# Causal masks of an attention with heads of 64: from mask matmuls to a masked maximum on VectorE and a select on GpSimd

## The chip, the cores and the metric

One core of one Trainium2 chip runs the whole program in a single launch. The metric is the device time of that launch in microseconds (us). The kernel before has three timed runs: 3772.35, 3780.45 and 3801.22 us, with a median of 3780.45. Apart from these, one execution was profiled, and every row of a profile in this document belongs to such an execution.

The engines are named as in the profile: PE is TensorE's matmuls, PEld its weight loads, DVE is VectorE, ACT is ScalarE, POOL is GpSimd, SP issues most of the DMAs.

## The reference

The program is four transformer layers on 2048 tokens of 128 channels, each of them half a feed-forward layer, an attention, and another half of the feed-forward layer. Attentions 0 and 3 are causal. The change is about attention 3: 16 heads of 64 over all 2048 tokens, keys and values made from a latent of 64, rotary embedding on queries and keys.

```python
q = jnp.einsum('bsd,qd->bsq', x, wq).reshape(B, S, H, D).transpose(0, 2, 1, 3)
kv_latent = jnp.einsum('bsd,ld->bsl', x, w_kv_down)
k = jnp.einsum('bsl,ql->bsq', kv_latent, w_k_up).reshape(B, S, H, D).transpose(0, 2, 1, 3)
v = jnp.einsum('bsl,ql->bsq', kv_latent, w_v_up).reshape(B, S, H, D).transpose(0, 2, 1, 3)
q = q * cos + _rotate_half(q) * sin
k = k * cos + _rotate_half(k) * sin
scores = jnp.einsum('bhsd,bhtd->bhst', q, k) / jnp.sqrt(jnp.float32(D))
causal = jnp.triu(jnp.full((S, S), -jnp.inf, dtype=jnp.float32), k=1)
scores = scores + causal[None, None]
probs = jax.nn.softmax(scores.astype(jnp.float32), axis=-1).astype(q.dtype)
out = jnp.einsum('bhst,bhtd->bhsd', probs, v)
```

Attention 0 has the same causal mask on 8 heads of 16, and matters here because it already carries its mask in the other way.

## The kernel before

All attentions run through one routine, `flash`. The 2048 tokens are four chunks of 512 (`CH`), each of four tiles of 128. Attention 3 takes its heads in pairs (`nh` is 2), so an iteration is one pair of heads and one chunk of queries, 8 pairs by 4 chunks, 32 iterations, in the order of `its`: all four chunks of a pair, then the next pair. A causal iteration of query chunk `qc` sees key chunks 0 to `qc`. The last of them is the diagonal one, and needs the mask.

An iteration has two passes, written as two generators.

- `stream_a` finds the maximum of every query's scores. For each tile `r` of 128 queries and each key chunk it multiplies queries by keys (L1045) for two heads into one double bank of PSUM (`first_pass_bank`, tag `s1`, two buffers), and VectorE reduces both halves in one `tensor_reduce` (L1068). On the diagonal chunk only `w` = 128, 256, 384 or 512 columns are made. The maxima are then put, negated, into rows of the query tile, so that the second pass's matmul subtracts them.
- `stream_b` makes the scores again, transposed, one tile of 128 keys against 512 queries at a time (L1150, two matmuls per head), ScalarE takes the exponential from PSUM into a tile `pt` in SBUF (L1159), and TensorE multiplies it by the values (`pv`, L1114). On the four diagonal key tiles the columns start at `c0` = 0, 128, 256 or 384, and the 128 columns from `c0` hold the triangle. The values of a key tile are emitted only after the scores of the next one, to give the exponential time. The first of these matmuls also waits for the last exponential by a manual dependency (`last_exp`), so that all the pair's exponentials are there.

How the sum of exponentials is made differs by attention. In attention 3 `on_exp` (L1965) adds every `pt` into a running sum for its head: the first head of the pair on GpSimd and the second on VectorE, and both on VectorE for the last two key tiles of an iteration. After the iteration, ones are multiplied by the sums (L1978), and the inverse travels through DRAM to scale the output (L1994, L2008).

The order of the work on TensorE is written out by hand. `pe(...)` keeps its matmuls in program order, and the main loop of `flash` decides after every yielded piece of `stream_b` how far `stream_a` may be ahead, counted in columns (`leads`, `knots`). So the maxima of coming iterations lie between the exponentials and values of the present one. `fill` adds pieces of the projections of coming pairs in between: TensorE products (L227 to L229, L1698, L1699), rotary products on VectorE (L1734) and rotary additions on GpSimd (L1744, L1750). VectorE and GpSimd have in-order queues whose order a scheduler sets; the reductions of the first pass have high priority in it.

The mask. `tiled` is true in the attentions whose heads are packed into strips of the array (0, 1 and 2), and false in attention 3. Where it is true and the attention is causal (attention 0), L1060 adds a strip, 384 columns of zeros and then the triangle, in the instruction that takes the maximum, and L1161 zeroes the triangle of `pt` with a select on GpSimd. Where it is false (attention 3), a matmul of the identity by a triangle of -1e30 in bfloat16 adds the mask into PSUM: L1049 in the first pass (`maskq_b`) and L1155 in the second (`maskk_b`).

```python
masked = last and not tiled
...
if masked:
    pe(nc.tensor.matmul(
        ps[:, o + w - P : o + w], masks_b["ident_b"],
        masks_b["maskq_b"], start=False, stop=True,
    ))
```

Of the kernel before, what the change touches and what calls it, by code (L numbers as in the profile page):

```python
# [9 lines left out]
F32 = mybir.dt.float32  # L10
# [17 lines left out]
E = 8  # L28
# [20 lines left out]
    (COLS, [("rb1", 4), ("rb2", 4), ("eb1", 4 * E), ("ln_scale", 1), ("ln_bias", 1),  # L49
            ("w1_s", 4), ("w2_s", 4), ("h1_s", 4), ("h2_s", 4), ("hscale", 1)]),  # L50
    (ROWS, [("rb3", E), ("b_proj", C), ("bias2", C), ("w3_s", C)]),
    (CONSTS, [("ident", P), ("before", P), ("maskq", P), ("maskk", P), ("least", E * E),
              ("ecap", TC * E), ("iota", P), ("iotaj", NJ), ("tile", NC * 2 * TC), ("spare", NJ), ("tok", 1),
              ("geo", P)]),
)
# [9 lines left out]
def tile_macaron(ctx: ExitStack, tc: tile.TileContext, a: dict, out: bass.AP, stages=STAGES):  # L65
# [35 lines left out]
    def cs(name):  # L101
        return cst[:, slice(*CONSTS[name])]
# [99 lines left out]

    def make_constants(other):
        for name, src in (
            ("ident_b", ident), ("maskq_b", cs("maskq")), ("maskk_b", cs("maskk")),
            ("before_b", cs("before")), ("ones_b", ones),
        ):
            masks_b[name] = const.tile([P, P], BF16, name=name)
            in_order(nc.vector.tensor_copy(masks_b[name], src), other)
        masks_b["ident_r"] = const.tile([P, P], F32R, name="ident_r")  # L210
        in_order(nc.vector.tensor_copy(masks_b["ident_r"], ident), other)
# [758 lines left out]
    def flash(io, pool, early, its, nh, causal, scale, s1, s2, pv_mm, put_max, begin, finish, poll=None,  # L970
# [20 lines left out]
        def pe(ins):  # L991
            return tc.keep_in_program_order(ins)
# [4 lines left out]
        def chunks(qc):  # L997
            return qc + 1 if causal else NC

        if tiled and causal:  # L1000
            junk = pool.tile([P, CH], F32, name="junk")
            strip = pool.tile([P, CH], F32, name="strip")
            nc.gpsimd.memset(strip[:, : CH - P], 0.0)
            nc.vector.tensor_copy(strip[:, CH - P :], cs("maskq"))
# [20 lines left out]
        def stream_a():  # L1025
            for n, (g, qc) in enumerate(its):
                begin(n)
                nk = chunks(qc)
                npair = (nk + 1) // 2
                mp = pool.tile([P, TC, nh, NC], F32, name="mp", tag="mp", bufs=3)  # L1030
                for pi in range(npair):
                    for r in range(TC):
                        before = hook(n, pi, r) if hook is not None else None
                        if pi == r == 0 and before is None:
                            before = last_top.get(n - 1)
                        for kc in range(2 * pi, min(2 * pi + 2, nk)):
                            for j0 in range(0, nh, 2):
                                ps = first_pass_bank()
                                last = causal and kc == qc
                                masked = last and not tiled  # L1040
                                w = (r + 1) * P if last else CH
                                for j in range(2):
                                    o = j * CH
                                    lhsT, rhs = s1(n, j0 + j, r, kc)
                                    pe(nc.tensor.matmul(  # L1045
                                        ps[:, o : o + w], lhsT, rhs[:, :w], start=True, stop=not masked
                                    ))
                                    if masked:
                                        pe(nc.tensor.matmul(  # L1049
                                            ps[:, o + w - P : o + w], masks_b["ident_b"],  # L1050
                                            masks_b["maskq_b"], start=False, stop=True,
                                        ))
                                    pos[0] += w
                                    if not tiled:
                                        yield w
                                both = ps.rearrange("p (j n) -> p j n", j=2)
                                with tc.high_priority():
                                    if last and tiled:
                                        for j in range(2):
                                            ins = nc.vector.tensor_tensor_reduce(  # L1060
                                                junk[:, :w], both[:, j, :w], strip[:, CH - w :], 1.0, NEG,
                                                ALU.add, ALU.max, mp[:, r, j0 + j, kc : kc + 1],
                                            )
                                            if before is not None:
                                                in_order(ins, before)
                                                before = None
                                    else:
                                        ins = nc.vector.tensor_reduce(  # L1068
                                            mp[:, r, j0 : j0 + 2, kc], both[:, :, :w], AX.X, ALU.max,
                                        )  # L1070
                                if before is not None:
                                    in_order(ins, before)
                                    before = None
                                if tiled:
                                    yield 2 * w
                mx = pool.tile([P, TC, nh], F32, name="mx", tag="mxa", bufs=3)
                nc.vector.tensor_reduce(mx, mp[:, :, :, :nk], AX.X, ALU.max, negate=True)
                put, last_top[n] = put_max(n, mx, pe)

                def done(n=n, put=put):  # L1080
                    put()
                    ready.add(n)

                after(2000.0, done)

        def stream_b():
# [45 lines left out]
            for n, (g, qc) in enumerate(its):  # L1132
# [5 lines left out]
                for kt in range(nt):  # L1138
                    at[1] = kt
                    c0 = CH - width(kt, qc)  # L1140
                    diag = causal and kt >= qc * TC
                    pts = {}
                    for at_j, j in enumerate(order):
                        if alive[0] or at_j % 2:
                            ps = bank("s2")
                        else:
                            ps = first_pass_bank()[:, :CH]
                        terms = s2(n, j, kt)
                        for i, (lhsT, rhs) in enumerate(terms):
                            pe(nc.tensor.matmul(  # L1150
                                ps[:, c0:], lhsT, rhs[:, c0:],
                                start=i == 0, stop=i == len(terms) - 1 and (tiled or not diag),
                            ))
                        if diag and not tiled:
                            pe(nc.tensor.matmul(  # L1155
                                ps[:, c0 : c0 + P], masks_b["ident_b"], masks_b["maskk_b"], start=False, stop=True
                            ))
                        pt = early.tile([P, CH], F32, name="pt", tag="pt", bufs=2 * nh + 2)
                        ex = nc.scalar.activation(pt[:, c0:], ps[:, c0:], AF.Exp, scale=scale)  # L1159
                        if diag and tiled:  # L1160
                            ex = nc.gpsimd.affine_select(  # L1161
                                pt[:, c0 : c0 + P], pt[:, c0 : c0 + P], [[1, P]], ALU.is_ge, 0.0,
                                base=0, channel_multiplier=-1,
                            )
                        pts[j] = pt
                        if on_exp is not None:
                            on_exp(n, kt, j, pts, c0)
                        if len(terms) > 1:
                            step((CH - c0) * (len(terms) - 1))
                        yield CH - c0  # L1170
                        if tiled and alive[0]:
                            if at_j % 2:
                                values(at_j // 2)
                        elif at_j == (split_at if alive[0] else nh - 1):
                            values()
                    if pv is None:
                        pv = held("pv")
                    pend[0] = (n, kt, nt, c0, pts, pv, ex)
                    if not alive[0]:
                        io.lead(2.3)  # L1180
# [940 lines left out]
def _constants():  # L2121
# [3 lines left out]
    def put(name, v):  # L2125
        c[:, slice(*CONSTS[name])] = v
# [2 lines left out]
    put("ident", np.eye(P))  # L2129
    put("before", i[:, None] < i[None, :])  # L2130
    put("maskq", np.where(i[None, :] > i[:, None], NEG, 0.0))
    put("maskk", np.where(i[:, None] > i[None, :], NEG, 0.0))
    e = np.arange(E)
    put("least", np.where(e[None, :] < e[:, None], 0.0, 2.0**-126).reshape(1, -1))
    put("ecap", np.tile(e * CAP - SLOTS - (P - 1) / 2.0, TC)[None, :])
# [130 lines left out]
```

## Time and profile before

| What | us |
|---|---|
| median of the timed runs (lowest, highest) | 3780.45 (3772.35, 3801.22) |
| profiled execution, device time | 3774.4 |
| its span in the trace | 3772.5 |
| attention 0, masked maxima on VectorE, first to last | 188.4 to 421.1 |
| attention 0, selects on GpSimd, first to last | 211.4 to 458.5 |
| attention 3, first to last mask matmul of the first pass | 2615.3 to 3586.4 |
| attention 3, first to last mask matmul of the second pass | 2637.5 to 3624.7 |
| PE busy in the span | 3463.1 |
| DVE busy in the span | 2858.9 |
| ACT busy in the span | 2075.1 |
| POOL busy in the span | 838.8 |

The device time and the span differ by 1.9 us, which lies around the span. The mean granted clock of TensorE over the span is 0.943 of full speed.

Matmul rows overlap each other: a row's length is the way of one matmul through the array, and the next begins before it ends. So busy time on PE says how long something was in the array, and what a matmul takes from the stream is read from the distance of two starts. A wait is put down to the releaser that came last. A chain of waits is followed back from the last instruction to what released it, and its shares say which lines the end of the program hung on.

### The profile page before, as it was taken

The page shows a single profiled execution, that of the slowest core. Times are in us where ns is not written, and L with a number is a line of the kernel's source. Part 1 is how long each engine was busy: PE and PEld are TensorE (multiplying, and loading weights), DVE is VectorE, ACT ScalarE, POOL GpSimd, SP SyncE. Part 2 cuts the span into 40 slices and gives each one's busy share as a digit, 9 for nine tenths or more (in the row PEclk, how much of TensorE's full clock was granted, in tenths as well). Part 3 has the DMA queues.
Part 4 walks back from the last instruction along what each step waited for, and adds up shares of the span by engine and source line. Part 5 has one row for each costly group of instructions (what it writes and reads, how often), then busy time and mean ns, then how long its engine had stood idle before and what let it go on. Part 6 is the DMA issues. An engine that isn't in the chain of part 4 may idle for free.

```text
span 3772.5 us, 61601 instructions
## 1 busy us (share of the span) xinstructions
PE 3463.1 (92%) x23613; PEld 1894.5 (50%) x23613; DVE 2858.9 (76%) x4794; ACT 2075.1 (55%) x3858; POOL 838.8 (22%) x860
## 2 busy tenths in 40 slices
PE   7689988978999999997999999888899999999999
PEld 5543366853333333883333333376455555555458
DVE  6578556768999996778899999654787777777762
ACT  3246732316888888331788888732344444444442
POOL 1511124010000000111000000144665444532341
PEclk9779989988999999995899999999999999999999
DMA  3410023000000000101000000013653343322110
GB/s 104 94 49 19 28 67 93 1 26 7 16 6 15 7 4 1 35 15 56 10 14 8 14 5 4 15 45 88 187 181 102 104 127 117 119 63 61 29 34 12
DMA packets 135015, 186.65 MB, mean 49 GB/s; under 512 B 27520, under 2 KB 54658, under 8 KB 134720
## 3 DMA queue, kind: packets, MB, share of 16 engines
q1 hardware_dynamic: 132160, 177.46, 15.9%
q0 software_dynamic: 2560, 5.25, 0.9%
q8 instruction: 186, 3.05, 0.3%
q14 instruction: 109, 0.89, 0.1%
HBM read 117.89 MB, written 45.87 MB: 43 GB/s over the span
## 4 chain that ended last, share of the span: by engine, by line
PE 68%; DVE 9%; ACT 4%; POOL 3%; issue 3%; DMA 2%; SPq 0%; DVEq 0%; POOLq 0%; ACTq 0%
PE pv L1114 21%; PE s L1150 20%; PE s L1045 4%; DVE mp L1068 4%; PE pd L725 3%; ACT pt L1159 2%; PE bank L227 2%; PE bank L228 2%; PE bank L229 2%; PE sums L1978 1%; PE bank L922 1%; PE pu L227 1%; PE pu L228 1%; PE py L2014 1%; PE pu L229 1%
## 5 line engine op out<-in xcount | busy, mean ns | idle before, releaser
L1159 ACT ACTIVATE pt<-s 128x512 f32<-128x512 f32 x3008 | 1552.4, 586 | 640.8 <-PE s L1150 401.6
L1068 DVE TENSOR_REDUCE mp<-s 128x2 f32<-128x1024 f32 (+3 forms) x1440 | 1630.1, 1183 | 161.8 <-PE s L1045 116.5
L1114 PE MATMUL pv<-pt,v 128*32 128x256 f32 (+5 forms) x9848 | 1053.8, 439 | 23.6 <-ACT ov L1528 11.3
L1150 PE MATMUL s<-q,km 32*128 32x512 f32 (+2 forms) x2368 | 746.9, 501 | 26.0 <-ACT pt L1159 16.3
L1045 PE MATMUL s<-km,qt 32*128 32x512 f32 (+3 forms) x2368 | 631.2, 517 | 55.4 <-DVE mp L1068 34.9
L1150 PEld LDWEIGHTS s<-q,km 32*128 32x128 f32 (+1 forms) x2368 | 328.4, 188 | 546.7 <-issue 352.0
L1114 PEld LDWEIGHTS pv<-pt,v 128*32 128x32 f32 (+1 forms) x9848 | 234.0, 112 | 394.1 <-issue 203.2
L143 POOL TENSOR_TENSOR rs<-rs,minus_half 128x4 f32<-128x4 f32 x56 | 58.7, 1048 | 1544.9 <-DVE rs L142 1544.1
L1150 PE MATMUL s<-q,k 128*128 128x512 f32 (+3 forms) x1280 | 387.3, 395 | 10.0 <-DVE rot L1734 7.0
L1150 PEld LDWEIGHTS s<-q,k 128*128 128x128 f32 x1280 | 210.8, 190 | 204.0 <-issue 100.1
L1965 DVE TENSOR_TENSOR sum<-sum,pt 128x512 f32<-128x512 f32 (+3 forms) x328 | 249.9, 772 | 81.2 <-ACT pt L1159 77.7
L1965 POOL TENSOR_TENSOR sum<-sum,pt 128x512 f32<-128x512 f32 (+1 forms) x200 | 260.0, 1300 | 217.6 <-ACT pt L1159 200.4
L1045 PEld LDWEIGHTS s<-km,qt 32*128 32x128 f32 (+1 forms) x2368 | 240.8, 195 | 118.1 <-DVE mp L1068 78.7
L1045 PE MATMUL s<-k,q 128*128 128x512 f32 (+3 forms) x640 | 237.5, 405 | 19.8 <-DVE mp L1068 15.7
L715 ACT ACTIVATE sg<-pg 128x1024 f32<-128x1024 f32 x72 | 73.9, 1027 | 174.4 <-PE pg L229 158.9
L1045 PEld LDWEIGHTS s<-k,q 128*128 128x128 f32 x640 | 124.0, 196 | 64.1 <-DVE mp L1068 23.2
L725 PEld LDWEIGHTS pd<-l1d,h 128*128 128x128 f32 x1152 | 139.3, 192 | 5.6
L725 PE MATMUL pd<-l1d,h 128*128 128x128 f32 x1152 | 140.1, 275 | 0.0
L717 DVE TENSOR_TENSOR h<-pu,sg 128x1024 f32<-128x1024 f32 x72 | 87.9, 1220 | 60.3 <-PE pu L229 55.3
L1734 DVE TENSOR_TENSOR rot<-rot,tab 128x512 f32<-128x512 f32 x128 | 87.4, 685 | 53.0 <-PE rot L1699 21.7
L1744 POOL TENSOR_TENSOR rot<-rot,rot 128x512 f32<-128x512 f32 x64 | 89.4, 1397 | 115.5 <-DVE rot L1734 101.4
L908 ACT ACTIVATE f<-bank,cols 128x512 f32<-128x512 f32 x64 | 44.1, 689 | 115.5 <-PE bank L229 109.5
(569 smaller groups left out, 4462.4 us busy)
## 6 DMA issues: line engine op xcount, KB each, us to landing
tab<-in_l3rope SPq DMA_DIRECT2D x66, 256.0 KB
q<-q SPq DMA_DIRECT2D x128, 128.0 KB
k<-k SPq DMA_DIRECT2D x64, 256.0 KB
l0e<-in_l0e SPq DMA_DIRECT2D x32, 256.0 KB
q<-h SPq DMA_DIRECT2D x32, 256.0 KB
q<-rot SPq DMA_DIRECT2D x32, 256.0 KB
k<-h SPq DMA_DIRECT2D x32, 256.0 KB
k<-rot SPq DMA_DIRECT2D x32, 256.0 KB
```

The source lines that it names most:

```text
L227: nc.tensor.matmul(ps, wh, xh, start=start, stop=False)
L228: nc.tensor.matmul(ps, wh, xl, start=False, stop=False)
L229: nc.tensor.matmul(ps, wl, xh, start=False, stop=stop)
L717: nc.vector.tensor_tensor(h.rearrange("p m n -> p (m n)"), pu, sg, ALU.mult)
L725: nc.tensor.matmul(pd[:, i, :], h[:, m, i * P : (i + 1) * P], wd[:, m, :], start=m == 0, stop=m == 1,)
L1045: pe(nc.tensor.matmul(ps[:, o : o + w], lhsT, rhs[:, :w], start=True, stop=not masked))
L1068: ins = nc.vector.tensor_reduce(mp[:, r, j0 : j0 + 2, kc], both[:, :, :w], AX.X, ALU.max,)
L1114: i = pe(nc.tensor.matmul(pv[out_rows, lo:hi], lhsT, pts[j][:, lo:hi], start=kt == 0, stop=kt == nt - 1 and hi == CH))
L1150: pe(nc.tensor.matmul(ps[:, c0:], lhsT, rhs[:, c0:], start=i == 0, stop=i == len(terms) - 1 and (tiled or not diag),))
L1159: ex = nc.scalar.activation(pt[:, c0:], ps[:, c0:], AF.Exp, scale=scale)
L1744: nc.gpsimd.tensor_tensor(f, f, halves[1].bitcast(F32), ALU.add)
L1965: eng.tensor_tensor(t[:, c0:], other[:, c0:], pts[j][:, c0:], ALU.add)
```

## The change

In every causal attention, attention 3 included, the diagonal chunk of the first pass is now reduced by one `tensor_tensor_reduce` per head (add the strip, take the maximum) in place of the mask matmul and the paired `tensor_reduce`, and the triangle of a diagonal `pt` is zeroed by GpSimd's `affine_select` after the exponential in place of the mask matmul before it. The values and the sums then depend on the select. The score matmuls close their own accumulation. The scratch output `junk` of the maximum becomes bfloat16 instead of float32, for attention 0 as well. The constant `maskk`, and the bfloat16 copies of both masks, are gone.

```diff
-    (CONSTS, [("ident", P), ("before", P), ("maskq", P), ("maskk", P), ("least", E * E),
+    (CONSTS, [("ident", P), ("before", P), ("maskq", P), ("least", E * E),
...
-            ("ident_b", ident), ("maskq_b", cs("maskq")), ("maskk_b", cs("maskk")),
+            ("ident_b", ident),
...
-        if tiled and causal:
-            junk = pool.tile([P, CH], F32, name="junk")
+        if causal:
+            junk = pool.tile([P, CH], BF16, name="junk")
             strip = pool.tile([P, CH], F32, name="strip")
             nc.gpsimd.memset(strip[:, : CH - P], 0.0)
             nc.vector.tensor_copy(strip[:, CH - P :], cs("maskq"))
...
-                                masked = last and not tiled
                                 w = (r + 1) * P if last else CH
...
-                                        ps[:, o : o + w], lhsT, rhs[:, :w], start=True, stop=not masked
+                                        ps[:, o : o + w], lhsT, rhs[:, :w], start=True, stop=True
                                     ))
-                                    if masked:
-                                        pe(nc.tensor.matmul(
-                                            ps[:, o + w - P : o + w], masks_b["ident_b"],
-                                            masks_b["maskq_b"], start=False, stop=True,
-                                        ))
...
-                                    if last and tiled:
+                                    if last:
                                         for j in range(2):
                                             ins = nc.vector.tensor_tensor_reduce(
                                                 junk[:, :w], both[:, j, :w], strip[:, CH - w :], 1.0, NEG,
...
-                                start=i == 0, stop=i == len(terms) - 1 and (tiled or not diag),
-                            ))
-                        if diag and not tiled:
-                            pe(nc.tensor.matmul(
-                                ps[:, c0 : c0 + P], masks_b["ident_b"], masks_b["maskk_b"], start=False, stop=True
+                                start=i == 0, stop=i == len(terms) - 1,
                             ))
                         pt = early.tile([P, CH], F32, name="pt", tag="pt", bufs=2 * nh + 2)
                         ex = nc.scalar.activation(pt[:, c0:], ps[:, c0:], AF.Exp, scale=scale)
-                        if diag and tiled:
+                        if diag:
                             ex = nc.gpsimd.affine_select(
                                 pt[:, c0 : c0 + P], pt[:, c0 : c0 + P], [[1, P]], ALU.is_ge, 0.0,
                                 base=0, channel_multiplier=-1,
                             )
...
-    put("maskk", np.where(i[:, None] > i[None, :], NEG, 0.0))
```

## The prediction

> **What bounds the kernel now.** I read the page first, then windows of each engine over the attention with 16 heads of 64 (2600 to 3640 us), the chain of waits there, the groups by shape, the waits, and a timeline of TensorE. Only that attention uses the edited branches; the earlier causal attention, 16 wide, already runs the new code and serves as a price list.
>
> From the page, then the chain of that stretch (shares of it), then three windows (pair of heads 4, query chunks 0 to 2 and chunk 3; pair 6, chunks 0 to 2; columns: length, PE, PEld, DVE, ACT, POOL busy, granted clock, DMA share, GB/s):
>
> ```profile
> PE 3463.1 (92%) x23613; PEld 1894.5 (50%) x23613; DVE 2858.9 (76%) x4794; ACT 2075.1 (55%) x3858; POOL 838.8 (22%) x860
> ...
> by line: PE s L1150 26.7%; PE pv L1114 23.7%; PE s L1045 12.2%; issue 4.9%; DVE mp L1068 3.3%; PE sums L1978 2.8%; PE py L2014 2.6%; DVE sum L1965 1.8%; PE s L1155 1.4%; PE rot L1698 1.4%; PE s L1049 1.3%; PE rot L227 1.2%; PE rot L229 1.1%
> ...
> 3183.00:3257.00 74.00, 72.57 (x365) 40.75 (x366) 59.49 (x88) 32.20 (x64) 30.82 (x25) 1.00 0.33 100
> 3257.00:3302.00 45.00, 45.00 (x210) 22.57 (x208) 34.15 (x49) 22.65 (x44) 28.45 (x21) 1.00 0.51 154
> 3414.00:3483.00 69.00, 67.43 (x343) 36.89 (x345) 50.36 (x78) 30.85 (x60) 18.11 (x15) 1.00 0.20 55
> ```
>
> See that TensorE is the bound at full granted clock, that the mask matmuls (L1049, L1155) are 2.7% of the chain of some 1040 us, so about 28 us, and that VectorE, 73 to 80% busy, is the runner-up: its maxima and sums already take 5.1%.
>
> The prices, groups by shape; L1060, L1161 and the accumulator read are from the 16-wide attention (190 to 480 us), the rest from 2640 to 3640 us (columns: count, busy us, mean ns, idle before, its releaser):
>
> ```profile
> L1155 PE MATMUL s<-maskk_b,ident_b 128*128 128x128 bf16 x255 | 58.7, 230 | 0.0
> L1049 PE MATMUL s<-maskq_b,ident_b 128*128 128x128 bf16 x240 | 53.9, 230 | 0.0
> L1068 DVE TENSOR_REDUCE mp<-s 128x2 f32<-128x1024 f32 x218 | 264.0, 1221 | 78.6 <-PE s L1045 68.3 <-PE s L1049 8.8
> L1068 DVE TENSOR_REDUCE mp<-s 128x2 f32<-128x256 f32 x30 | 12.3, 411 | 0.0
> L1060 DVE CUSTOM_DVE_ANT_0 junk<-s,strip 128x512 f32<-128x512 f32 x32 | 22.0, 688 | 3.9 <-PE s L1150 2.2 <-PE s L1045 0.3
> L1060 DVE DVE_READ_ACCUMULATOR2_ANT mp<- 128x1 f32 x126 | 10.4, 82 | 0.0
> L1060 DVE CUSTOM_DVE_ANT_0 junk<-s,strip 128x128 f32<-128x128 f32 x30 | 8.6, 286 | 1.0
> L1161 POOL TENSOR_SCALAR_AFFINE_SELECT pt<-pt 128x128 f32<-128x128 f32 x128 | 36.3, 294 | 190.4 <-ACT pt L1159 189.2
> L1965 POOL TENSOR_TENSOR sum<-sum,pt 128x512 f32<-128x512 f32 x168 | 226.0, 1345 | 173.8 <-ACT pt L1159 171.4
> L1965 DVE TENSOR_TENSOR sum<-sum,pt 128x512 f32<-128x512 f32 x168 | 171.9, 1023 | 45.3 <-ACT pt L1159 45.0
> ```
>
> A mask row's 230 ns is latency. What it takes from the stream is the distance between starts, in the timeline of TensorE (start, length):
>
> ```profile
> 3123.30 0.40 PE L1045 MATMUL s<-k,q 128*128 128x512 f32 x1
> 3123.54 0.23 PE L1049 MATMUL s<-maskq_b,ident_b 128*128 128x128 bf16 x1
> 3123.58 0.59 PE L1150 MATMUL s<-q,k 128*128 128x384 f32 x2
> ...
> 3133.63 0.23 PE L1049 MATMUL s<-maskq_b,ident_b 128*128 128x128 bf16 x1
> 3133.79 1.08 PE L1114 MATMUL pv<-pt,v 128*64 128x512 f32 x4
> ...
> 3215.14 0.39 PE L1045 MATMUL s<-k,q 128*128 128x512 f32 x1
> 3215.46 0.44 PE L1114 MATMUL pv<-pt,v 128*64 128x128 f32 x4
> ```
>
> A mask before a score matmul costs 0.04 us, before the values (pv) 0.16; without one, score to pv takes 0.32 where score, mask, pv takes 0.24 + 0.16 = 0.40.
>
> **The change, part by part.** 8 pairs of heads by 4 query chunks are 32 iterations, each with 8 masks in the first pass (4 row tiles, 2 heads) and 8 in the second (4 diagonal key tiles, 2 heads): 512 mask matmuls go, with their weight loads. 119 of them stand before a pv: 119 x 0.08 = 9 us. The other 393 at 0.04 to 0.05: 17 us. Sum 26 us, near the chain's 28. [...]
>
> Added on VectorE: each of 128 paired TENSOR_REDUCEs becomes two masked maxima with two accumulator reads. At 512 columns 2 x (0.688 + 0.082) = 1.54 against 1.22; at 128, 2 x (0.286 + 0.082) = 0.74 against 0.41; the two shapes between likewise. So 0.32 us more each, 128 x 0.32 = 41 us. Cover: VectorE's 20 to 27% of idle, and the first half can begin one score matmul earlier (0.24 us). Behind a longer maximum stand sums and the next maximum, and TensorE waits for the first-pass bank (two buffers). Of L1068's time the chain holds 3.3% of 1040 = 34 us out of 325 busy, a tenth; I put a fifth of 41 on the path: 8 us, ends 0 and 41.
>
> Added on GpSimd: 256 selects of 0.294 us, 75 us more where it is busy some 40 to 63%. The select stands between exponential and both users, pv and the sum. For pv I laid every diagonal exponential beside its pv in the trace: between the end of the second head's exponential and the pv start, medians are 3.2, 2.9, 1.5 and 1.5 us for the four diagonal tiles, and a quarter of the last have under 0.8 (least 0.05). A select needs some 0.5 us with handovers (my estimate; the traced select waits 0.1 or so for its ACT row), up to 1.3 us more behind a GpSimd sum. Shortfall: about 0.3 us on 16 of the last tiles and less on some others, near 5 us; another 5 for backlog, when GpSimd's head of queue holds a sum or rotary add that waits for VectorE (rows: 73.7 us waited for L2008 in 7 places, longest 18.5; they fall at key tile 1 of chunk 1, just ahead of its selects). 10 us, ends 2 and 40.
>
> The sums: 200 adds of diagonal tiles are on VectorE (the last two tiles always, the second head before). Setting max(end of exponential, end of the GpSimd instruction then running) plus 0.5 us against each add's traced start, VectorE would stand a further 90 us in all. Queued behind are maxima, and rotary products that GpSimd itself awaits. The chain holds 1.8% = 19 us of the sums' time, a fourteenth; waiting is less evenly buffered, so I take an eighth: 12 us, ends 0 and 90.
>
> [...]
>
> With one answer, zero: the strip's memset and copy (1 to 2 us on GpSimd and VectorE, ahead of a stage that opens with DMA waits; uncovered, +2); maskk's 64 KB and two casts at the start (beside loads of weights, -0.5 at most); the bfloat16 junk in the 16-wide attention (the input is still float32 in PSUM; between -5 and +5 for 128 rows); SP's queue and the order of TensorE's remaining work (unchanged in the text).
>
> Sum: -26 + 8 + 10 + 12 = +4 us on the profiled execution's 3774.4 (span 3772.5), 3778; that execution lies 6 below the median of 3780.45, so 3785 on the runs' scale.
>
> **The rivals.** *All cover holds.* Every addition hides in slack and only the masks' time shows: 3780 - 26 = 3754. For it: the medians of slack, VectorE's idle quarter. Against: TensorE already waits for L1068 and both cover engines are in order.
>
> *Convoy on VectorE.* Its adds wait for selects, selects stand behind 1.3 us GpSimd sums, and the maxima behind the adds leave TensorE without a first-pass bank. Place: the diagonal tiles of chunks 1 and 2, where maxima for the next chunk are made. Price: half of 90 + half of 41 + 20 for pv - 26 = +60, so 3840. It decides once 0.25 us or so of each add's wait reaches TensorE (200 x 0.25 = 50, with 8 + 10 - 26 = +42). For it: 101 waits of L1965 for an exponential exist already (79.0 us). Against: two banks and the idle quarter.
>
> *The masks were free.* If TensorE only waits elsewhere instead of 26 us saved, the additions stand alone: +10 to +30, 3800. For it: the page's PE ends are modelled; against: the chain counts the masks.
>
> **How the numbers follow.** Small net change 0.45, cover holds 0.22, convoy 0.22, masks free 0.11. About 1% (38 us) is what a measurement of this kernel can tell. A gain past it needs more than all masks cost, 0.04. A loss past it is most of the convoy and a bit of the others, 0.23; the rest, 0.73, within. Range: 3752 (cover holds) to 3830 (the near half of the convoy).
>
> **What would show it.** Right: L1049 and L1155 gone, L1060 at 0.69 us for 512 columns in this attention, selects near 0.3 us, VectorE some 40 us busier, and the attention within 10 us of its old length. The convoy would show as L1965 on VectorE waiting for POOL pt, and longer waits of PE s L1045 for DVE mp. The forecast is wrong if pv waits for POOL pt by tens of us, if selects take over 0.6 us, or if the stage shortens by over 30 us.

## The result, and the profile after

The changed kernel takes 3837.03 us (median of 4 runs, 3832.82 to 3839.96). The kernel before, with one more run on the same chip, has a median of 3783.44. The ratio is 1.0136, with a 95% interval of 1.0095 to 1.0178: slower, with the whole interval above 1, and above the range that was forecast.

First the page of the changed kernel and its chain of waits from 2600 to 3700 us, cut by the view at its line length, then windows over the same work as before: pair 4, chunks 0 to 2 and chunk 3, and pair 6, chunks 0 to 2.

```profile
PE 3460.7 (90%) x23101; PEld 1889.9 (49%) x23101; DVE 2866.5 (75%) x5177; ACT 2072.5 (54%) x3858; POOL 917.7 (24%) x1117
...
by line: PE s L1144 22.2%; PE pv L1108 19.6%; PE s L1044 9.8%; POOL sum L1955 5.4%; issue 4.8%; DVE mp L1062 3.3%; PE sums L1968 2.8%; DVE sum L1955 2.6%; POOL rot L1734 2.4%; POOL pt L1151 2.4%; PE py L2004 1.9%; DVE rot L1724 1.7%; POOL r
...
3232.00:3313.00 81.00, 71.08 (x319) 40.13 (x319) 62.85 (x125) 31.85 (x63) 36.96 (x46) 0.96 0.30 92
3313.00:3360.00 47.00, 45.11 (x193) 22.96 (x191) 32.56 (x63) 23.18 (x45) 33.20 (x34) 0.96 0.50 148
3472.00:3543.00 71.00, 64.40 (x299) 34.66 (x297) 52.93 (x112) 30.61 (x60) 24.54 (x36) 1.00 0.19 52
```

Three things changed. GpSimd, which had no line among the first of the chain, now holds over 10% of it (sum, rot, pt). TensorE is busy 88% of the first window where it was 98%. And the granted clock is 0.96 in both windows of pair 4, which was 1.00.

Attention 3 itself is best measured from its first pv matmul to its last, in the group of pv matmuls of before and of the changed kernel (columns: shortest, median and longest duration in ns, then start of the first and of the last):

```profile
L1114 PE MATMUL pv<-pt,v x1280: 272/592/1116, 2652.3 to 3625.5; 128*64 128x512 f32 x129, 128*64 128x256 f32 x19, 128*64 128x384 f32 x18, 128*64 128x128 f32 x17
```

```profile
L1108 PE MATMUL pv<-pt,v x1280: 272/592/1116, 2667.5 to 3686.4; 128*64 128x512 f32 x129, 128*64 128x256 f32 x19, 128*64 128x384 f32 x18, 128*64 128x128 f32 x17
```

That is 973.2 us before and 1018.9 after, 45.7 longer. Taken by pair of heads from the same starts, pairs 0 to 4 lost 17.8, 3.5, 6.1, 6.7 and 8.8 us; pairs 5 to 7, where the rotary work of later pairs is done and GpSimd is lighter, lost 2.9 together.

The new rows in attention 3 (groups by shape, 2640 to 3700 us) have the prices read from attention 0, but for the select, at 352 ns where it took 294 there:

```profile
L1151 POOL TENSOR_SCALAR_AFFINE_SELECT pt<-pt 128x128 f32<-128x128 f32 x256 | 87.7, 352 | 186.9 <-ACT pt L1149 183.2 <-DMA q<-q 2.5
L1054 DVE CUSTOM_DVE_ANT_0 junk<-s,strip 128x512 bf16<-128x512 f32 x62 | 42.4, 684 | 18.4 <-PE s L1044 18.1
L1054 DVE DVE_READ_ACCUMULATOR2_ANT mp<- 128x1 f32 x248 | 20.0, 81 | 0.0
L1054 DVE CUSTOM_DVE_ANT_0 junk<-s,strip 128x128 bf16<-128x128 f32 x62 | 17.4, 281 | 0.4 <-PE s L1044 0.2
L1955 POOL TENSOR_TENSOR sum<-sum,pt 128x512 f32<-128x512 f32 x168 | 224.4, 1336 | 151.6 <-ACT pt L1149 146.7 <-DMA k<-k 1.8
```

Of these, only the masked maxima and the selects are new work, and they are of the lengths that were priced, the select's 58 ns more making 15 us over 256 of them. The rest of the loss is looked for in waits: first those of the kernel before (2640 to 3640 us), then of the changed one (2640 to 3700 us); columns: total us, times, longest.

```profile
DVE sum L1965 <- ACT pt L1159: 79.0, 101, 2.0
PEld s L1045 <- DVE mp L1068: 20.2, 28, 2.4
PEld L1939 <- DVE top L1932: 9.6, 5, 3.0
PEld pv L1114 <- ACT pt L1159: 7.1, 20, 1.1
```

```profile
DVE sum L1955 <- POOL pt L1151: 84.8, 89, 3.2
PEld s L1044 <- DVE mp L1062: 32.9, 36, 3.4
PEld s L1044 <- DVE mp L1054: 30.9, 26, 4.4
DVE sum L1955 <- ACT pt L1149: 29.4, 39, 2.0
PEld L1929 <- DVE top L1922: 24.1, 13, 5.8
PEld pv L1108 <- POOL pt L1151: 22.3, 32, 3.7
```

The waits of TensorE's weight loads for maxima tripled (20 to 64 us), those for the written maxima (top) more than doubled, and a wait of pv for the select is new (22.3 us). VectorE's sums, which waited 79 us for exponentials, now wait 114 in all, 85 of it for the select.

One place shows how these hang together. It is the changed kernel's timeline at chunk 1 of pair 2 (start, length; in brackets the idle time before and its releaser):

```profile
2992.68 2.96 POOL L1955 TENSOR_TENSOR sum<-sum,pt 128x512 f32<-128x512 f32 x2
2992.81 0.94 PE L2004 MATMUL py<-l3o,ov 128*128 128x128 f32 x7
2992.90 0.49 ACT L1149 ACTIVATE pt<-s 128x384 f32<-128x384 f32 x1
...
2995.59 0.29 POOL L1151 TENSOR_SCALAR_AFFINE_SELECT pt<-pt 128x128 f32<-128x128 f32 x1
2995.85 1.26 POOL L1955 TENSOR_TENSOR sum<-sum,pt 128x512 f32<-128x512 f32 x1
2997.07 0.29 POOL L1151 TENSOR_SCALAR_AFFINE_SELECT pt<-pt 128x128 f32<-128x128 f32 x1
2997.39 1.34 DVE L1955 TENSOR_TENSOR sum<-sum,pt 128x384 f32<-128x384 f32 x1 [2.27 <-POOL pt L1151]
2998.66 0.68 DVE L1054 CUSTOM_DVE_ANT_0 junk<-s,strip 128x512 bf16<-128x512 f32 x1
2999.26 0.68 DVE L2007 TENSOR_TENSOR x<-x,py 128x512 f32<-128x512 f32 x1
3000.00 0.51 PE L1144 MATMUL s<-q,k 128*128 128x256 f32 x2 [3.88 <-DVE x L2007]
```

The exponential ends at 2993.39. Its select begins at 2997.07, 3.7 us later, behind three full-width sums of GpSimd. VectorE stands 2.27 us at the sum that needs this select, with a masked maximum and the addition of an earlier output (L2007) behind it. The matmuls for that addition (L2004) ended at 2993.75, so it could have run in the pause, but it stands later in the queue. TensorE stands 3.88 us for the PSUM bank that this addition frees. The clock record then has TensorE at half clock (0.50 granted) for 6.8 us from 3000.7.

### The profile page after: what moved, and what is told of

Its sections match the earlier page's. It is cut to its first block, busy times and chain, and to the rows that moved or that the text cites. A ratio compares the mean times of both kernels' runs of the same rounds, so it can differ in the third digit from the quotient of the medians.

```text
span 3834.2 us, 61095 instructions
## 1 busy us (share of the span) xinstructions
PE 3460.7 (90%) x23101; PEld 1889.9 (49%) x23101; DVE 2866.5 (75%) x5177; ACT 2072.5 (54%) x3858; POOL 917.7 (24%) x1117
## 4 chain that ended last, share of the span: by engine, by line
PE 64%; DVE 11%; POOL 5%; ACT 4%; issue 2%; DMA 1%; SPq 0%; POOLq 0%; DVEq 0%; ACTq 0%
PE pv L1108 20%; PE s L1144 19%; DVE mp L1062 4%; PE s L1044 4%; PE pd L725 3%; ACT pt L1149 2%; PE bank L227 2%; PE bank L228 2%; PE bank L229 2%; POOL sum L1955 2%; PE sums L1968 1%; POOL rot L1734 1%; PE bank L922 1%; DVE sum L1955 1%; PE pu L227 1%
## 5 line engine op out<-in xcount | busy, mean ns | idle before, releaser
L1062 DVE TENSOR_REDUCE mp<-s 128x2 f32<-128x1024 f32 x1312 | 1529.8, 1218 | 142.8 <-PE s L1044 118.8
L1108 PE MATMUL pv<-pt,v 128*32 128x256 f32 (+5 forms) x9848 | 1071.0, 446 | 34.9 <-POOL pt L1151 15.9
L1955 DVE TENSOR_TENSOR sum<-sum,pt 128x512 f32<-128x512 f32 (+3 forms) x328 | 239.7, 740 | 113.9 <-POOL pt L1151 84.8
L1955 POOL TENSOR_TENSOR sum<-sum,pt 128x512 f32<-128x512 f32 (+1 forms) x200 | 256.9, 1285 | 154.1 <-ACT pt L1149 146.7
L1044 PE MATMUL s<-k,q 128*128 128x512 f32 (+3 forms) x640 | 225.5, 391 | 46.3 <-DVE mp L1054 21.8
L1054 DVE CUSTOM_DVE_ANT_0 junk<-s,strip 128x256 bf16<-128x256 f32 (+3 forms) x384 | 186.0, 484 | 50.8 <-PE s L1044 40.8
L1151 POOL TENSOR_SCALAR_AFFINE_SELECT pt<-pt 128x128 f32<-128x128 f32 x384 | 123.9, 332 | 375.2 <-ACT pt L1149 370.3
```

Source lines behind the costliest of these rows:

```text
L1044: pe(nc.tensor.matmul(ps[:, o : o + w], lhsT, rhs[:, :w], start=True, stop=True))
L1054: ins = nc.vector.tensor_tensor_reduce(junk[:, :w], both[:, j, :w], strip[:, CH - w :], 1.0, NEG, ALU.add, ALU.max, mp[:, r, j0 + j, kc : ...
L1062: ins = nc.vector.tensor_reduce(mp[:, r, j0 : j0 + 2, kc], both[:, :, :w], AX.X, ALU.max,)
L1108: i = pe(nc.tensor.matmul(pv[out_rows, lo:hi], lhsT, pts[j][:, lo:hi], start=kt == 0, stop=kt == nt - 1 and hi == CH))
L1151: ex = nc.gpsimd.affine_select(pt[:, c0 : c0 + P], pt[:, c0 : c0 + P], [[1, P]], ALU.is_ge, 0.0, base=0, channel_multiplier=-1,)
L1955: eng.tensor_tensor(t[:, c0:], other[:, c0:], pts[j][:, c0:], ALU.add)
```

## The experiments

Each kernel was compared with the kernel before on the same chip; a ratio is against those runs. "Attention 3" is first to last pv in the profiled execution. The kernel before gave 973.2 and, in a second profile, 976.6; the changed kernel 1018.9 and 1023.4. So the two pairs of profiles of this stage repeat within 5 us, and smaller differences are not read. The other rows rest on one profile each.

| Attention 3 has | ratio (95% interval) | attention 3, us |
|---|---|---|
| before: masks by matmul in both passes | 1 | 973.2, 976.6 |
| no mask at all (e15_bare) | 0.9968 (0.9958 to 0.9978) | 957.3 |
| first-pass masks left out (e18_topfree) | 0.9949 (0.9929 to 0.9969) | 963.5 |
| first pass as changed, second as before (e1_first) | 1.0017 (1.0000 to 1.0033) | 975.7 |
| all mask matmuls, masked maximum too (e16_max) | 1.0035 (1.0025 to 1.0046) | 983.9 |
| masked maximum, no mask in the second pass (e6_nomask) | 1.0024 (1.0010 to 1.0038) | 984.0 |
| the same, select into scratch (e8_apart) | 1.0075 (1.0046 to 1.0104) | 995.5 |
| e8_apart, sums wait for it (e10_apart_sum) | 1.0111 (1.0070 to 1.0152) | 1011.9 |
| e8_apart, pv waits for it (e9_apart_pv) | 1.0095 (1.0059 to 1.0131) | 1018.9 |
| first pass as before, second as changed (e2_second) | 1.0090 (1.0061 to 1.0119) | 1012.0 |
| all mask matmuls, select too (e17_select) | 1.0115 (1.0080 to 1.0151) | 1011.9 |
| all mask matmuls, masked maximum and select too (e7_kept) | 1.0111 (1.0083 to 1.0139) | 1014.9 |
| changed | 1.0136 (1.0095 to 1.0178) | 1018.9, 1023.4 |
| changed, rotary additions on VectorE (e5_rot) | 1.0096 (1.0067 to 1.0125) | 1012.3 |
| changed, tops first (e13_tops) | 1.0126 (1.0103 to 1.0150) | 1015.3 |
| changed, triangle zeroed by VectorE (e3_vector) | 1.0135 (1.0108 to 1.0161) | 1018.6 |
| changed, diagonal sums on GpSimd (e12_sums) | 1.0167 (1.0150 to 1.0184) | 1036.1 |

**Which half of the change.** Two kernels make half of it each (their cuts are shown against the kernel before), two the whole of it with GpSimd relieved (shown against the changed kernel).

```diff
  e1_first: first pass of the change only (mask of the second by matmul, operands exchanged)
-        masked = last and not tiled
+        masked = False
-        if last and tiled:
+        if last:
```

> First pass as changed (masked maximum on VectorE), second pass as before (mask matmul on TensorE, with the triangle as weights and the identity as moving operand; the geometry constants come by a DMA of their own to make room). Attention 3 from first to last pv took 973.2 us before and 1018.9 changed. If selects on GpSimd carry the loss: attention 3 within 960 to 980 here, and PE's waits for masked maxima (L1054 in the changed kernel, 30.9 + 21.8 us) fall under 20. If the longer VectorE work carries it: 1000 to 1020. If only both together lose: 975 to 990. Time of the whole, with the stage before attention 3 as in the kernel before (no theory foresees its half clock): 3765 to 3785, or 3810 to 3835.

```diff
  e2_second: second pass of the change only
-        if diag and not tiled:
-            pe(nc.tensor.matmul(... masks_b["maskk_b"] ...))
-        if diag and tiled:
+        if diag:
```

> Second pass as changed (select on GpSimd, no mask matmul), first pass as before (mask matmul, paired maximum). If selects on GpSimd carry the loss: attention 3 at 1000 to 1020 us from first to last pv, pairs 0 to 4 longer by 30 or more together and pairs 5 to 7, which have no rotary additions on GpSimd, by 3 at most. If the longer maxima carry it: 960 to 980. Sums on VectorE wait for the select by some 80 us either way.

The first pass changed costs nothing in attention 3 (975.7); the second pass carries the loss (1012.0, pairs 0 to 4 longer by 32.7 and pairs 5 to 7 by 6.0, where 3 at most were expected). So the longer maxima are not the main cause.

```diff
  e3_vector: in attention 3
-        ex = nc.gpsimd.affine_select(pt[:, c0 : c0 + P], ...)
+        ex = nc.vector.tensor_tensor(pt[:, c0 : c0 + P], pt[:, c0 : c0 + P], cs("tri"), ALU.mult)
```

> The changed kernel, with the triangle of attention 3 zeroed on VectorE by a product with zeros and ones, 128 columns, in place of the select on GpSimd (geometry constants by a DMA of their own for room). If waiting in GpSimd's queue is the cost: attention 3 at 965 to 995 us though VectorE gets 256 products more of about 0.25 us (64 us). If VectorE's load is the cost: 1020 to 1050, slower than the changed kernel.

```diff
  e5_rot: L1734 of the changed kernel
-        nc.gpsimd.tensor_tensor(f, f, halves[1].bitcast(F32), ALU.add)
+        nc.vector.tensor_tensor(f, f, halves[1].bitcast(F32), ALU.add)
```

> The changed kernel, with the 64 rotary additions of queries and keys (1.37 us each on GpSimd) on VectorE (about 0.7 us each). If GpSimd's queue is the cost: selects behind rotary additions go, attention 3 falls from 1018.9 to 985 to 1005, all of it in pairs 0 to 4. If VectorE's load is the cost: 1025 to 1045.

Neither theory had e3_vector right: out of GpSimd's queue the step costs as much as in it (1018.6), though VectorE had 256 products more to do there, so the run does not rule out GpSimd's queue. Freeing GpSimd of rotary additions brings 7 to 11 us, less than expected of a queue that is the whole cause. What the versions share is one more instruction between the exponential and its users.

**The dependency, or the work.** Four kernels on the changed one, all without an effective mask in the second pass.

```diff
  e6_nomask
-        if diag:
+        if diag and tiled:
             ex = nc.gpsimd.affine_select(pt[:, c0 : c0 + P], ...)
  e8_apart adds, for attention 3
+        shade = nc.gpsimd.affine_select(apart, pt[:, c0 : c0 + P], ...)
  e9_apart_pv adds
+        ex = shade
  e10_apart_sum adds, in place of that, a dependency of every diagonal sum on shade
```

> The changed kernel with nothing masked in the second pass of attention 3: no mask matmul, no select (left out: the triangle of the exponentials there). If the loss is the step between the exponential and its users, or GpSimd's load: attention 3 between first and last pv at 950 to 968 us, against 973.2 before and 1018.9 changed. If it comes from what is removed (TensorE without these matmuls has pauses, or the order of the queues shifts): 1000 to 1020.

> As the run without a mask, with a select of the same size on GpSimd for each diagonal tile that reads the exponentials and writes a scratch tile, so nobody waits for its result (left out: the mask in the second pass of attention 3). If the dependency is the cost: 950 to 975 us for attention 3. If GpSimd's added 75 us of work, its port or the order of its queue is the cost: 1000 to 1020.

> The scratch select of the run before, and the pv matmuls wait for the second head's select as in the changed kernel; the sums do not (left out: the mask in the second pass of attention 3). If TensorE's own wait for the select carries the loss: 995 to 1015 us for attention 3. If VectorE's waiting sums and what is queued behind them carry it: 960 to 980.

> The scratch select, and the sums of diagonal tiles wait for their select as in the changed kernel; the pv matmuls do not (left out: the mask in the second pass of attention 3). If VectorE's waiting sums carry the loss: 995 to 1015 us for attention 3, with PE waiting for maxima by 80 us or more. If TensorE's own wait carries it: 960 to 980.

The work alone, awaited by nobody, takes 11.5 us (984.0 to 995.5). The wait of pv brings 23 more, the wait of the sums 16 more, and the changed kernel, with both, is where the first of them already is. The run with waiting sums met its side's range, the one with waiting pv came out 4 us above its own, so the two are not rivals: either wait is enough for most of the loss. e8_apart fell between its two ranges (975 and 1000), and no run tells the causes that its second range names apart. And e6_nomask missed: with nothing but the masked maximum left of the change, and 512 matmuls fewer, it should have been under 968.

**Putting the new work elsewhere.**

```diff
  e12_sums
-        late = kt >= 4 * its[n][1] + 2
-        eng = nc.vector if late or count[0] % SHARE == 0 else nc.gpsimd
+        own = kt >= 4 * its[n][1]
+        eng = nc.gpsimd if own or count[0] % 3 == 0 else nc.vector
  e13_tops
+        with tc.high_priority():
             nc.vector.tensor_reduce(mx, ...)
             put, last_top[n] = put_max(n, mx, pe)
```

> The changed kernel once more, on the chip of this group, as the measure for the other three: 1.3% slower than before, attention 3 from first to last pv at 1010 to 1025 us, and TensorE at half clock for 50 us or more of it (10 us before, 68 changed).

> The changed kernel; the sums of all diagonal tiles are on GpSimd, behind their selects in the same queue, and of the other sums only every third is (every second before), so VectorE never waits for a select. If the loss is VectorE standing at such a sum with maxima, tops and projections behind it: attention 3 falls from 1018.9 to 970 to 995 us. If it is pv waiting for the select or GpSimd's load: 1010 to 1035, since GpSimd gets busier.

> The changed kernel; the last maximum of a chunk and the two writes of its halves (mx, top) have the high priority of the maxima, so that the scheduler places them ahead of waiting sums. If the order of VectorE's queue, set by estimates that the change altered, is a large part: PE's wait for top (38 us changed, 16 before) under 15 us, attention 3 at 995 to 1008. If other waits take its place: 1012 to 1022.

The second profile of the changed kernel met its expectation. Sums beside their selects on GpSimd do free VectorE (its sums waited 84.8 us for the select; only the copies of chunk 0 still do, 17.1 us), and the wait moves to pv: PE's weight loads wait 64.4 us for the select there (22.3 changed), and attention 3 is the longest of all. Tops first lowers the wait for top from 24 to 18 us and gains no more than two profiles differ by.

> The changed kernel with the mask matmuls of the second pass left in as well as the select (masked twice there, same result). If the mask matmuls cost TensorE about what their starts say (256 x 0.05 = 13 us): attention 3 at 1028 to 1038 us. If they were hidden in waits, or if their removal is what lowers the clock: 1000 to 1020.

The kernel of e7_kept has the mask matmuls of both passes left in, not of the second alone as its expectation says, so the dearer theory would have put it near 1045. It came to 1014.9, not longer than the changed kernel: 512 matmuls more do not lengthen attention 3 there.

**Each part by itself, TensorE's work kept.** The three kernels are the kernel before, with both mask branches taken out (e15_bare), with `if last:` for the masked maximum (e16_max, its second-pass mask with operands exchanged as in e1_first), and with `if diag:` for the select (e17_select).

> The kernel before without any mask in attention 3: the 512 mask matmuls are gone and nothing takes their place, the maxima are the paired ones of before (left out: the causal mask of attention 3's diagonal tiles). If the masks cost TensorE the 26 us that the distances of starts gave: attention 3 at 943 to 955 us against 973.2. If they lay in time in which TensorE waits for other engines anyway: 966 to 978.

> The kernel before, all mask matmuls kept, and the masked maximum on VectorE beside them (the result is the same; geometry constants by a DMA of their own for room). The price of the 41 us of VectorE alone: attention 3 at 974 to 985 us if it is mostly covered, as the run with the first pass alone makes likely; 990 or more if it is not.

> The kernel before, all mask matmuls kept, and the select on GpSimd after the exponential beside them. The price of the select alone: attention 3 at 1000 to 1015 us if the step between exponential and users carries the loss whatever TensorE does; 980 to 990 if it bites only where TensorE has been made shorter.

> The kernel before, for a second profile: attention 3 at 970 to 978 us and half clock in it for under 20 us, if the profile of before was typical. The first half clock of attention 1 (51 us in the profile of before, 109 changed, in a stage the change does not touch) comes out anywhere from 50 to 110 if it is chance, near 51 if it belongs to the program.

These settle the sum, against 975 for before: the masks' removal alone is worth 18 us, the masked maximum alone costs 9, the select alone 37. Added up that is 28; the change lost 46. The missing 18 is the masks' gain itself, which is there when nothing else is changed (957.3) and gone when the select is there (1011.9 with the masks, 1012.0 without those of the second pass). Where it went is in the waits. Summed over attention 3 between first and last pv, PE's weight loads stand for VectorE 61 us before, 95 without masks, 117 with the masked maximum as well (e6_nomask), 130 changed; in the kernels with all masks kept they stand 77 (e16_max), 78 (e17_select) and 87 (e7_kept). A shorter TensorE meets VectorE earlier. Windows from first to last pv show it in TensorE's own time (before, bare, select beside the masks, changed; the granted clock is the third value from the end):

```profile
2652.00:3626.00 974.00, 938.38 (x4529) 503.10 (x4529) 737.19 (x1075) 441.53 (x841) 453.24 (x349) 0.99 0.35 105
```

```profile
2680.00:3638.00 958.00, 901.13 (x4036) 486.85 (x4035) 736.87 (x1074) 438.39 (x840) 455.89 (x349) 0.98 0.35 106
```

```profile
2677.00:3690.00 1013.00, 953.95 (x4531) 511.78 (x4529) 721.04 (x1076) 441.56 (x841) 523.01 (x602) 0.98 0.33 101
```

```profile
2667.00:3687.00 1020.00, 922.71 (x4038) 496.66 (x4038) 743.61 (x1436) 439.17 (x841) 532.02 (x602) 0.97 0.33 100
```

What a window has beyond PE's busy time, TensorE stood idle: 36 us before, 57 bare, 59 with the select beside the masks, 97 changed. Without the masks TensorE is busy 37 us less, and gives 21 of them back standing. From the select beside the masks to the changed kernel it is busy 31 us less and idle 38 more: there the masks' gain went.

The clock has a part in it too. Its record has half clock for 10 and 20 us of attention 3 before, 31 bare, 38 in each of the kernels with select and all masks, 68 and 90 changed. The bare and the changed kernel run the same matmuls, and the changed one is busy with them for 22 us more, with 37 us more of half clock. So the 46 us lost are 62 more of idle time, 37 less of masks, and some 20 more for the lower clock (an estimate from these rows).

**A version that beats both.** The mask of the maximum isn't needed for the result: a maximum over the unmasked scores is at least the masked one, and the softmax divides the surplus out again as long as it is far inside the range of float32. It is less robust where masked scores lie far above the others.

```diff
  e18_topfree: kernel before
-        masked = last and not tiled
+        masked = False
  e19_topfree_both: also
-        if last and tiled:
+        if False:
```

> The kernel before without the 256 first-pass mask matmuls of attention 3, paired maxima as before, second pass as before. The maximum then runs over all scores of the diagonal tiles and is at least the masked one, which a softmax allows while the surplus stays far from the range of float32; no part of the mask is left out. From the run without masks, where 512 matmuls were worth 16 to 19 us: attention 3 at 964 to 972 us, 0.1 to 0.4% faster than before. If the gain turns into waits for VectorE again: 972 to 978 and no difference.

> The same, and attention 0 too takes its maxima over unmasked scores with the paired reduction in place of the masked maximum: 64 rows of VectorE become 0.32 us shorter there, 20 us in a stage where VectorE is busy for 75 to 82 of 94 us. If VectorE sets the pace there: 5 to 15 us faster than the run before it. If TensorE does: within 4 us of it.

Both beat the kernel before. Attention 3 is 963.5 us in the first, 10 to 13 shorter, just past the short end of what was expected. The whole gained more than expected (0.51%, some 19 us, with 12 to 27 in the interval); what is beyond attention 3 is not explained. The second is at 0.9927 (0.9903 to 0.9951), which overlaps the first. In its profile attention 0 takes 235.8 us from first to last pv, where the other profiles have 237.1 to 245.2. So the masked maximum may cost attention 0 a few us, and one profile doesn't show it.

## Why the prediction was wrong

The forecast was 3785 us, 3752 to 3830, most likely within 1%. Measured: 3837, 1.36% slower. Two terms of its sum failed. In attention 3 it had -26 for the masks, +8 for the maxima and +22 for the select, +4 in all. The two additions came to +40 together (e7_kept, 1014.9 against 975), 9 and 37 each alone, where 30 were put; and taking the masks out beside them gained nothing (1018.9 and 1023.4), where 26 were put. By its steps:

- *The masks, 26 us gained.* This step failed by the most: the time was counted as saved whatever the other engines do. Alone the masks are worth 16 to 19 in attention 3 (957.3 against 973.2 and 976.6), less than the distances of starts, which count as gain also what TensorE then waits. Beside the select they are worth nothing that two profiles can tell (1011.9 against 1012.0, 1014.9 against 1018.9), since the busy time saved comes back as idle time (31 us less busy, 38 more idle). So the rival that the masks were free held beside the select, and did not hold alone.
- *The masked maximum, 41 us on VectorE and 8 on the path.* Right: 9 us with the masks kept, nothing net in e1_first, where it stands against 256 matmuls.
- *The select, 10 us through pv and 12 through the sums.* This is the other step that failed. Alone the select costs 37 us (e17_select). By parts, on the kernel without an effective mask: its work with nobody waiting took 11.5 us (984.0 to 995.5), the wait of pv 23 more where 10 were put, the wait of the sums 16 more where 12 were; both waits together (1018.9 and 1023.4) are little more than either (1018.9, 1011.9).
- *The waits behind these two prices.* The two pieces of the select's own delay were put at 0.5 us and up to 1.3 behind one sum. Selects of the second head in the first two diagonal tiles begin 1.2 and 1.7 us after their exponential in the mean (0.07 where nothing is in the way), 3.7 in the example, and take 0.35 more. VectorE's further standing at its sums, put at 90 us, was only 35 (79 to 114); what was too small is the share of it that reached TensorE, put at an eighth. Behind the waiting sum stand maxima, tops and output additions, which TensorE awaits with longest waits of 4 to 6 us. The place was named, chunk 1, and there the timeline shows 3.88 us in a single wait. But the reason given for it went: GpSimd's sums waited 73.7 us for L2008 before, and 9.7 us for the same line (L1998) in the changed kernel.
- *Adding the parts up.* The sum took each part's cover as independent of the others. It isn't: the masked maximum costs 9 us with the masks there and 27 without any mask (957.3 to 984.0). TensorE without its masks has less to do while VectorE catches up.
- *The select's length.* The select averages 352 ns in attention 3, with 810 as the worst, against the 294 of attention 0 that it was priced with: 15 us of lengthening in all. Of the 48 selects over 400 ns, 38 lie beside a sum on VectorE (L1955), of the other 208 only 60; the 98 beside such a sum average 417 ns, the 158 others 311. What this is worth in attention 3's time, no run shows.

What happened has the signs of the convoy, which was given 0.22: sums on VectorE wait for the select, and TensorE waits longer for maxima. The sign against the forecast, pv waiting for the select by tens of us, came too (22.3). That its 3840 lies so near is in part luck: it had 45 for the sums, 20 for pv and 20 for the maxima, less 26 for the masks, where 37 for the select, 9 for the maxima and nothing for the masks were measured. The range stopped at its near half, and the grounds against more were the two banks and VectorE's idle quarter. That idle time was no cover: in the first window of pair 4 VectorE's busy share even fell, from 80 to 78%, while it held TensorE up.

Of the 62 us between the two profiled spans, 15 lie ahead of attention 3. They are put down to chance (next but one section).

## What to carry to other kernels

An instruction put between a producer and its users can cost far more than its work (here 11.5 us with nobody waiting for it, 28 to 35 with the sums or pv waiting): price what stands behind each waiting user in that user's queue, not only the wait of the user. Work removed from the busiest engine is worth its length only while no other engine is close behind (37 us of TensorE's busy time gave 16 to 19 us here); try the removal alone, leaving that part of the computation out, before paying for what replaces it. And ask first whether the work is needed: leaving the maximum unmasked made the kernel 0.5% faster with these scores, where moving its mask to VectorE gained nothing.

## What the hardware showed that was not expected

Attention 1 is the same in both kernels, yet there the two profiles part by 20 us: the drift between their pv starts is -2.2 us at 872 us and +17.4 at 919. The windows have the cause, the granted clock (third value from the end), first of before, then of the changed kernel:

```profile
860.00:880.00 20.00, 16.00 (x99) 5.75 (x97) 15.15 (x14) 10.84 (x20) 0.00 (x0) 0.68 0.00 0
880.00:900.00 20.00, 18.23 (x168) 6.70 (x171) 15.55 (x14) 14.69 (x29) 0.00 (x0) 1.00 0.03 8
```

```profile
878.00:898.00 20.00, 20.00 (x116) 5.83 (x108) 12.08 (x10) 10.35 (x20) 0.00 (x0) 0.50 0.00 1
898.00:918.00 20.00, 19.99 (x123) 6.25 (x123) 11.58 (x10) 10.30 (x21) 0.00 (x0) 0.50 0.04 11
```

TensorE is shown busy for all of 40 us at half clock and is not given the full one; the half clock lasted 51 us before and 109 changed. The second profile of the kernel before had 96 us of it, and its attention 3 begins at 2682.3 us where the first one's began at 2652.3. Four builds on one chip that do the same work there (e6, e8, e9, e10) had 92, 106, 51 and 92. So this length is taken for chance, and two profiles of the same program differ by 20 to 30 us: spans of single profiles are not to be compared without it. Timed runs show it too. The six runs of e19_topfree_both are three of 3742 to 3746 us with a mean granted clock of 0.947, and three of 3765 to 3771 with 0.937 to 0.940.

In attention 3 half clock is recorded beside TensorE's waits: each of its 12 stretches in the changed profile, 3.4 to 10.2 us long, begins within a pause of 1.1 to 5.1 us or up to 2.2 us after its end (the 3.88 us above is one). But 19 other pauses of over 1 us there have no half clock beside them, so a pause alone doesn't tell when it comes. The profiles of before have 3 and 5 stretches; the 3 of the first begin 0.5 to 1.3 us after pauses of 1.9 to 2.3 us.
